# A's masked products in one piece with B's and the state part, keys and slots an iteration sooner in seven steps, values and gates an iteration later

## The chip, the core and the metric

The kernel runs on one core of a Trainium2 chip. The metric is the device time of one execution in microseconds (us); lower is better. The core has five engines with queues of their own: TensorE (PE, with its weight loads shown apart as PEld), VectorE (DVE), ScalarE (ACT), GpSimd (POOL) and SyncE (SP, which issues DMAs here). Each engine takes its instructions in a fixed order; semaphores make one wait for another.

## What is computed

All data are float32. The program is a feed-forward layer with two experts, an attention with a slot memory (16 heads, key width 64, value width 128, 64 slots), and the same feed-forward layer again. The attention of one head, cut to what matters:

```python
z = cumlogsumexp(s, axis=time)            # s: clipped slot scores
p, g = exp(s - z), exp(z[t-1] - z[t])
hk = hk * g[None, :] + k[:, None] * p[None, :]   # key state, step by step
ok = q @ hk;  pv = softmax(ok)                   # over the 64 slots
hv = hv * g[:, None] + p[:, None] * v[None, :]   # value state
o = pv @ hv                                       # then normalised, gated, projected by Wo
```

Two sequences of 1024 tokens with 512 features come in; q, k, s, v and the gate are products of the normalised tokens with five weight matrices.

## The kernel before

The attention works in units: one batch, one group of 4 heads, one chunk of 128 tokens. There are 2 x 4 x 8 = 64 units, taken by a loop over `i` (line 1315 on). In iteration `i` three units are at work: `cur` (unit i) has its keys, slots and queries made, `mid` (unit i-1) has its attention worked out, and `old` (unit i-2) is projected. Before and after the loop stand the two feed-forward layers; the second one starts inside the last iterations.

For one unit the chunk form needs two masked 128 x 128 products for each head. A (line 1117, `scores`) is keys times queries, made at the end of the iteration in which the unit is `cur`, and used by `slot_scores` in the next iteration (PE tile `ok<-A,E`). B (line 1199, `slot_weights`) is slots times softmax weights, made while the unit is `mid`, and used by `outputs` (PE tiles `ov<-v,B` and `svp<-v,B`). Both contract over 64 rows only, so each matmul fills half of the array's rows (form `64*128`), and the two halves run side by side. Their results lie in PSUM tiles of the tag `at` (2 buffers), and DVE multiplies each by the causal mask (line 1114), which also moves it to SBUF. `state_outputs` (`ov<-sv,uT`, `svp<-sv,uT`) has the same half-height form. `value_state_products` (`svp<-v,E`) and the second part of `slot_scores` (`ok<-A,E`) write 64 of 128 columns (form `128*64`). All the rest is `128*128`.

Values with gates and keys with slots are products of 256 tokens (a pair of units) with a 512-row weight, each done as seven block products instead of eight, by sums of blocks made beforehand (a Winograd form). The sums of the tokens (`token_sums`, PE input X) are four DVE additions. Both are generators that are advanced a step at a time between the other work, by the letters handed to `project(even, odd)`: `values_gates` has six steps, `keys_slots` five. Keys of a pair are made in the even iteration of its first unit. The first four steps of values are made in the odd iteration before, the other two in the even iteration:

```python
            project("k", "v")      # then slot_scores(mid)
            project("k", "v")      # then transpose_out(old), slot_softmax(mid)
            project("kvk", "v")    # then transpose_u(mid), update_key_state(mid)
            project("vk", "v")     # then slot_weights(mid), state_outputs, value_state_products
```

After these come `transpose_keys_slots(cur)` (PE tile tk, copied to kET by ACT), `running_sum(cur)` (DVE scans CT and the reciprocal rC), `queries(cur)` every fourth unit (PE tile pq), `outputs(mid)`, `scores(cur)` and `project_out(old)` (PE tile po, added to x by DVE, line 1282).

The order of PE's instructions in the attention is written out by hand: `on_pe` (line 952) chains each matmul behind the one before. The other engines' orders and the choice of a buffer are made by a scheduler that goes by priorities; it makes an instruction wait for what its operands and its buffers need, and PSUM is guarded by whole banks of 2 KB per partition. Slots E have three buffers of one tag (line 1046), keys k two, the token sums X share six buffers with other sums. PSUM tiles of the tag `pj` have two: the projections kU, kV, C, V, pq and po take them in turn.

In `keys_slots` before, C (for the first key) and V share a bank (line 1054); V's first product follows U's second. The weights of a group are loaded by SP in iterations c=4 to 7 of the group before it (queries, values and gates, keys and slots, outputs), and the sums of the weights' blocks for the groups 1 to 3 are made by POOL during b=0 (`weight_sums`, twelve items, two steps an iteration).

Of the kernel before, what the change touches and what calls it, by code (L numbers as in the profile page):

```python
# [15 lines left out]
P = 128  # L16
# [33 lines left out]
def tile_macaron(  # L50
# [406 lines left out]
    def ffn(m, views):  # L457
# [140 lines left out]
        def hidden_fast(ps, ck, xT, T, wfc, S, a, sums):  # L598
            w = wfc.rearrange("p (k d h) -> p k d h", k=2, d=2)
            lo, hi = slice(0, 256), slice(256, 512)  # L600
            a += [None] * 4
            for q in range(2):
                nm = f"{ph}_{ps}_{ck}_{q}"
                first, second = ts(q, P), slice(256 + q * P, 256 + (q + 1) * P)
                U = ps2.tile([P, 256], F32, tag="pj", name=f"hU{nm}")
                V = ps2.tile([P, 256], F32, tag="pj", name=f"hV{nm}")
                C = ps1.tile([P, 256], F32, tag="st", name=f"hC{nm}")

                def product(bank, left, right, start):
# [6 lines left out]
                def keep(name):  # L616
                    t = work.tile([P, 256], F32, tag=name, name=f"{name}{nm}")
# [6 lines left out]
                p1 = keep("rC")  # L624
# [214 lines left out]
    class Attention:  # L839
# [19 lines left out]
        def weight_sums(self):  # L859
# [17 lines left out]

            def load(j):
                g, d = j // 3, j % 3
                if d == 2:  # L880
                    return load_w(w_ks[g], f"kw{g}")
                w = large_tile([P, 4, 512], f"gw{g}_{d}")
                for i, src in enumerate((w_v, w_g)):
                    nc.sync.dma_start(
                        out=w[:, 2 * i : 2 * i + 2, :],
                        in_=src[g].rearrange("p (k d n) -> p k d n", k=2, d=2)[:, :, d, :],
                    )
                return w

            w = None  # L890
            for j in range(3 * NG):
                g, d = j // 3, j % 3
                if w is None:
                    w = load(j)
                if d < 2:
                    parts = w[:, 0], w[:, 2], w[:, 1], w[:, 3]
                    to = vg_sums[g].rearrange("p (t d n) -> p t d n", t=4, d=2)[:, :, d, :]
# [47 lines left out]
    def attention(att, then, then_steps, weight_steps):  # L945
# [36 lines left out]
        def values_gates(u):  # L982
# [19 lines left out]

            product(U, a11, B11, True)
            p1 = keep(U, "th", "p1")
            token_sums(u)
# [24 lines left out]
        def keys_slots(u):  # L1030
            pair = u, units[u.n + 1]
            B11, B21, B22, T1, T2, T3, T4 = att.ks[u.b, u.g]
            a11, a12, a21, a22 = halves(u)
            U = ps2.tile([P, 256], F32, tag="pj", name=f"kU{u.nm}")

            def keep(bank, tag):
                t = work.tile([P, 256], F32, tag=tag, name=f"{tag}{u.nm}", bufs=1)
# [1 line left out]
                return t  # L1039

            def key(v):
                v.k = work.tile([P, HG * DK], F32, tag="k", name=f"k{v.nm}")
                return v.k

            def slot(v, bank, other):
# [2 lines left out]
                nc.vector.tensor_scalar(v.E, v.E, -32.0, 32.0, ALU.max, ALU.min)  # L1048
                nc.scalar.activation(v.E, v.E, AF.Exp)

            product(U, a11, B11, True)
            p1 = keep(U, "kp")

            bank = ps2.tile([P, 2, 256], F32, tag="pj", name=f"kV{u.nm}")
            C, V = bank[:, 0], bank[:, 1]
            product(C, a12, B21, True)
            nc.vector.tensor_tensor(key(u), C, p1, ALU.add)
            yield
            product(U, u.S[:, 1], T2, False)
            u2 = keep(U, "ku")  # L1060
            product(V, u.S[:, 0], T1, False)
            p5 = keep(V, "kv")
            yield
            product(V, u.S[:, 3], B22, False)
            slot(u, V, u2)
# [32 lines left out]
        def masked_products(u, name, lT, rT):  # L1098


            m = work.tile([P, HG, P], F32, tag="msk", name=f"{name}{u.nm}", bufs=3)
            pp = [
                ps2.tile([P, NPR, P], F32, tag="at", name=f"{name}p{u.nm}_{j}") for j in range(2)
            ]
            for pr in range(NPR):
                for j in range(2):
                    r = slice(j * 64, (j + 1) * 64)
                    on_pe(
                        nc.tensor.matmul,
                        pp[j][:, pr, :], lhsT=lT[r, pr, :], rhs=rT[r, pr, :],  # L1110
                        start=True, stop=True,
                    )
            for j in range(2):
                nc.vector.tensor_tensor(m[:, ts(j, NPR), :], pp[j], causal[:, 0:NPR, :], ALU.mult)  # L1114
            return m

        def scores(u):

            u.A = masked_products(
                u, "A", u.kET[:, 0:NPR, :], u.qT[:, :, ts(u.c % 4, P)]  # L1120
            )

        def running_sum(u, prev):

# [63 lines left out]
        def transpose_u(u):  # L1188
# [10 lines left out]
        def slot_weights(u):  # L1199

            u.Bm = masked_products(u, "B", u.kET[:, NPR:, :], u.uT)

# [94 lines left out]

        n = len(units)  # L1300
        norm = att.norm(1)
        ahead = keys = None

        def project_ahead(i):
            nonlocal ahead
            if ahead is None and i % 2 and i + 1 < n:
                ahead = values_gates(units[i + 1])
            if ahead is not None:  # L1310
                next(ahead)

        for _ in range(4):
            project_ahead(-1)
        for i in range(n + 2):
            cur = units[i] if i < n else None
            mid = units[i - 1] if 1 <= i <= n else None
            old = units[i - 2] if i >= 2 else None


            def project(even, odd):
                if i >= n - 1:
                    next(then_steps)
                for step in (odd if i % 2 else even) if cur else "":
                    if step == "v":
                        project_ahead(i)
                    else:
                        next(keys)

            if cur and i % 2 == 0:  # L1330
                keys = keys_slots(cur)
            project("k", "v")
            if mid:
                slot_scores(mid)
            project("k", "v")
            if old:
                transpose_out(old)
            if mid:
                slot_softmax(mid)
            project("kvk", "v")  # L1340
            if mid:
                transpose_u(mid)
                update_key_state(mid)
            project("vk", "v")
            with tc.issue_after(att.pe.ins):
                then.settle()
            if mid:
                slot_weights(mid)
                state_outputs(mid)
                value_state_products(mid)  # L1350
            if cur:
                transpose_keys_slots(cur)
                running_sum(cur, mid)
                queries(cur, mid)
            project("", "")
            if cur and i % 2 == 0:
                ahead = None
            if mid:
                outputs(mid)
                update_value_state(mid)  # L1360
# [1 line left out]
                if mid.b == 0 and mid.c < 6 and mid.g < NG - 1:  # L1362
                    with tc.issue_after(mid.gated.ins):
                        next(weight_steps)
                        next(weight_steps)
            if cur:
                scores(cur)
            if old:
                project_out(old)
            if cur:  # L1370
# [8 lines left out]
                if cur.c >= 4 and cur.n + NC < n:  # L1379
                    v = units[cur.n + NC]  # L1380
                    if cur.c == 4:
                        att.load_queries(v.b, v.g)
                    elif cur.c == 5:
                        att.load_values_gates(v.b, v.g)
                    elif cur.c == 6:
                        att.load_keys_slots(v.b, v.g)
                    else:
                        att.load_outputs(v.b, v.g)
                if cur.g == NG - 1 and cur.b == B - 1:
# [83 lines left out]
```

## Time and profile before

| what | value |
|---|---|
| median of 3 runs | 2323.75 us (2321.03 to 2326.47) |
| the profiled execution | 2324.62 us |
| its span (first to last instruction) | 2322.8 us |
| granted TensorE clock | 0.995 |
| 0 to 496 us (first layer) | PE busy 460.36, DVE 277.74 |
| 496 to 1800 us (attention) | PE busy 1287.17 of 1304.00, DVE 802.10, ACT 518.61, POOL 126.67 |
| 1800 to 2322 us (end of attention, second layer) | PE busy 496.69, DVE 275.66 |

The profile's page lists busy time by engine, the waits by who released whom, and the instructions in order of time. A row of the timeline has the start in us, the time from the first start to the last end in us, the engine, the line, the operation, output<-input, the form, and how many records are merged in it. A float32 matmul shows as two records, a transpose as one. The line of PE's attention work is always 954, that of the helper, so one goes by tiles. The end of a matmul is modelled: 128x512 records last 592 ns and follow each other every 429 ns, so the last 163 ns of each run beside the next one.

### The profile page before, as it was taken

How to read it: one execution, taken by the hardware profiler on the slowest of the kernel's cores; microseconds unless marked ns; L12 is line 12 of the kernel's file. 1: busy time of each engine (PE TensorE's matmuls, PEld its weight loads, DVE VectorE, ACT ScalarE, POOL GpSimd, SP SyncE). 2: the span in 40 equal slices, each digit the busy share in tenths (PEclk: the TensorE clock that was granted, in tenths of full speed). 3: DMA queues.
4: the chain of work that ended last, by engine and by line, in shares of the span. 5: the costliest groups of instructions: out<-in, count | busy, mean ns of one | idle time of the engine just before them, and what ended most of it. 6: DMA issues, size and time to landing. Idle time of an engine off the chain costs nothing.

```text
span 2322.8 us, 28879 instructions
## 1 busy us (share of the span) xinstructions
PE 2244.2 (97%) x10776; PEld 1542.2 (66%) x10776; DVE 1355.5 (58%) x3124; ACT 783.6 (34%) x1526; POOL 470.5 (20%) x400
## 2 busy tenths in 40 slices
PE   6999999999999999999999999999999999999998
PEld 5687787875656656556666655665655667888765
DVE  6544556656656656657765655655656666665411
ACT  2222222323344334334434443343433332222222
POOL 3523615301101101100101000000001245434000
PEclk9999999999999999999999999999999999999999
DMA  7516425231311311310411200210010203323442
GB/s 290 223 55 213 181 88 223 105 116 37 125 53 64 123 46 64 116 56 25 164 33 56 76 32 20 73 42 29 36 37 20 90 33 145 113 96 100 168 172 100
DMA packets 56940, 222.74 MB, mean 96 GB/s; under 512 B 5983, under 2 KB 13151, under 8 KB 38880
## 3 DMA queue, kind: packets, MB, share of 16 engines
q1 hardware_dynamic: 51232, 203.52, 24.7%
q0 software_dynamic: 5280, 16.85, 1.8%
q8 instruction: 85, 1.39, 0.2%
q10 hardware_dynamic: 288, 0.52, 0.1%
q14 instruction: 55, 0.45, 0.1%
HBM read 189.86 MB, written 31.54 MB: 95 GB/s over the span
## 4 chain that ended last, share of the span: by engine, by line
PE 67%; issue 12%; DVE 12%; POOL 3%; ACT 2%; DMA 2%; SPq 0%; POOLq 0%; DVEq 0%; ACTq 0%
PE U L954 8%; PE oa L678 6%; PE hU L611 6%; PE po L954 5%; PE o L678 4%; PE pq L954 4%; PE V L954 4%; PE hp L514 3%; PE op L733 3%; PE hV L611 3%; PE kV L954 3%; PE kU L954 2%; PE C L954 2%; DVE rC L1132 2%; PE svp L954 2%
## 5 line engine op out<-in xcount | busy, mean ns | idle before, releaser
L1240 POOL TENSOR_TENSOR sg<-sg,ms 128x512 f32<-128x512 f32 x64 | 69.0, 1077 | 1178.2 <-DVE ms L1238 1080.1
L954 PE MATMUL po<-wo,oT 128*128 128x512 f32 x512 | 236.7, 605 | 1.7 <-DVE A L1114 1.7
L954 PEld LDWEIGHTS po<-wo,oT 128*128 128x128 f32 x512 | 92.0, 189 | 101.3 <-issue 91.8
L514 PE MATMUL hp<-xsT,wfc 128*128 128x256 f32 (+1 forms) x768 | 148.9, 349 | 10.3 <-DMA wfc<-in_w_fc_dram 5.7
L514 PEld LDWEIGHTS hp<-xsT,wfc 128*128 128x128 f32 x768 | 127.5, 192 | 33.3 <-issue 13.7
L733 PE MATMUL op<-wp,a 128*128 128x512 f32 x320 | 143.2, 593 | 0.0
L1236 ACT ACT_TABLE_LOAD x63 | 80.8, 1283 | 176.7 <-DVE ms L1235 176.6
L501 DVE SCALAR_TENSOR_TENSOR t<-hp,r 128x256 f32<-128x256 f32 (+1 forms) x96 | 36.4, 379 | 154.6 <-ACT r L500 151.0
L954 PE MATMUL U<-vgT,X 128*128 128x512 f32 x256 | 120.7, 594 | 0.0
L1132 DVE RECIPROCAL rC<-CT 128x256 f32<-128x256 f32 x64 | 112.2, 1753 | 2.2
L954 PE MATMUL pq<-xnT,wq 128*128 128x512 f32 x256 | 112.5, 592 | 0.0
L611 PE MATMUL hU<-xsT,wfc 128*128 128x256 f32 x384 | 100.3, 383 | 0.4 <-ACT e L618 0.3
L733 PEld LDWEIGHTS op<-wp,a 128*128 128x128 f32 x320 | 59.7, 190 | 60.9 <-issue 57.9
L1233 DVE TENSOR_REDUCE ms<-sq 128x4 f32<-128x512 f32 x64 | 41.2, 644 | 78.2 <-ACT sq L1231 78.2
L500 ACT ACTIVATE r<-hp 128x256 f32<-128x256 f32 (+1 forms) x96 | 33.2, 347 | 155.4 <-PE hp L514 151.8
L954 PEld LDWEIGHTS pq<-xnT,wq 128*128 128x128 f32 x256 | 47.4, 190 | 53.6 <-issue 53.6
L611 PEld LDWEIGHTS hU<-xsT,wfc 128*128 128x128 f32 x384 | 72.4, 191 | 13.9 <-issue 3.0
L1165 ACT ACT_TABLE_LOAD x63 | 80.8, 1283 | 1.1
L954 PEld LDWEIGHTS U<-vgT,X 128*128 128x128 f32 x256 | 48.9, 191 | 47.9 <-issue 46.2
L1000 ACT ACTIVATE th<-sg 128x512 f32<-128x512 f32 x64 | 40.4, 631 | 112.8 <-DVE sg L998 108.3
L1127 DVE TENSOR_TENSOR_SCAN CT<-ones,CT,kET 128x128 f32<-128x128 f32 x112 | 48.1, 471 | 51.5 <-ACT kET L1096 51.5
L1269 ACT ACTIVATE oT<-to,gnh 128x512 f32<-128x512 f32 x64 | 44.0, 687 | 94.4 <-PE to L954 85.4
(302 smaller groups left out, 5146.9 us busy)
## 6 DMA issues: line engine op xcount, KB each, us to landing
wfc<-in_w_fc_dram SPq DMA_DIRECT2D x48, 1024.0 KB, 5.7
wp<-in_w_proj_dram SPq DMA_DIRECT2D x48, 1024.0 KB, 6.6
vgT<-vgs SPq DMA_DIRECT2D x16, 1024.0 KB, 5.9
wv<-in_w_v_dram SPq DMA_DIRECT2D x8, 1024.0 KB, 7.3
ksT<-kss SPq DMA_DIRECT2D x8, 1024.0 KB, 5.3
wo<-in_w_o_dram SPq DMA_DIRECT2D x8, 1024.0 KB, 4.8
xs<-xs SPq DMA_DIRECT2D x6, 1032.0 KB
wks<-in_w_ks_dram SPq DMA_DIRECT2D x24, 256.0 KB, 3.9
```

Source lines behind the costliest of these rows:

```text
L514: m.mark = nc.tensor.matmul(hp, lhsT=wfc[:, dc * HQ + hc * P : dc * HQ + (hc + 1) * P], rhs=xT[:, dc, :], start=(dc == 0), stop=(dc == DC ...
L611: m.mark = nc.tensor.matmul(bank, lhsT=left[:, d, :], rhs=right[:, d, :], start=start and d == 0, stop=d == 1, skip_group_check=True,)
L678: nc.tensor.matmul(bank[:, t, :], lhsT=left(q)[:, ts(t, P)], rhs=right(q), start=first and q == 0 and (t == 0 or last), stop=last and q == ...
L733: nc.tensor.matmul(ops[j], lhsT=a[hc][:, ts(j, P)], rhs=wp[:, ts(hc, D)], start=(ck == 0 and hc == 0), stop=(ck == NHQ - 1 and hc == HQ // ...
L954: att.pe = op(*args, **kw)
L1127: nc.vector.tensor_tensor_scan(u.CT[:, pr, :], ones, u.kET[:, NPR + pr, :], prev.CT[:, pr, P - 1 : P] if u.c else 0.0, ALU.mult, ALU.add,)
L1132: nc.vector.reciprocal(u.rC, u.CT)
L1165: nc.scalar.activation(u.u, u.u, AF.Exp)
L1233: nc.vector.tensor_reduce(ms, sq, AX.X, ALU.add)
L1236: nc.scalar.activation(ms, ms, AF.Sqrt, bias=eps, scale=1.0 / DV)
L1240: u.gated = then.gated = nc.gpsimd.tensor_tensor(sg, sg, ms.to_broadcast([P, HG, DV]), ALU.mult)
L1269: nc.scalar.activation(u.oT, tp, AF.Copy, scale=gnh)
```

## The change

- `masked_products` now makes B of `mid` and A of `cur` in one go: B's four products, the four of `state_outputs(mid)`, A's four products, then the four masks. A and B of the same half lie in one PSUM tile of 2 KB, so `at` still has two tiles. This happens once in an iteration, before `value_state_products(mid)`.
- For A to be there so soon, keys and slots of a pair are made in the odd iteration before it (`keys_slots(units[i + 1])`), in seven steps instead of five. Those of the first pair are made ahead of the loop, all seven steps in a row. `transpose_keys_slots` and `running_sum` are of unit i+1 now and stand at the end of the iteration; `queries(cur)` stands after the second `project`.
- Values and gates of a pair start in the even iteration of its first unit (four steps); their last two steps fall into the odd iteration after it.
- In `keys_slots` U and V share a bank, and C has its own. V's first product comes ahead of U's second. `token_sums` moves from the first step of values to the first step of keys. k has three buffers instead of two; E keeps three.
- In iterations c=5 and c=6 of a group the loads change places: keys and slots first. `weight_sums` takes the key-and-slot item of a group first. In the feed-forward layer p1 is kept in the tags `kp` and `kv`, one buffer each, instead of `rC`.

```diff
             product(U, a11, B11, True)
             p1 = keep(U, "kp")
-
-            bank = ps2.tile([P, 2, 256], F32, tag="pj", name=f"kV{u.nm}")
-            C, V = bank[:, 0], bank[:, 1]
+            token_sums(u)
+            yield
+            C = ps2.tile([P, 256], F32, tag="pj", name=f"kC{u.nm}")
             product(C, a12, B21, True)
             nc.vector.tensor_tensor(key(u), C, p1, ALU.add)
             yield
+            product(V, u.S[:, 0], T1, False)
+            p5 = keep(V, "kv")
+            yield
             product(U, u.S[:, 1], T2, False)
             u2 = keep(U, "ku")
-            product(V, u.S[:, 0], T1, False)
-            p5 = keep(V, "kv")
             yield
...
+            if u:
+                products(0, u.kET[:, NPR:, :], u.uT)
+                state_outputs(u)
+            if v:
+                products(1, v.kET[:, 0:NPR, :], v.qT[:, :, ts(v.c % 4, P)])
+            if u:
+                u.Bm = mask(0, "B")
+            if v:
+                v.A = mask(1, "A")
...
-            project("k", "v")
+            project("v", "kk")
             if mid:
                 slot_scores(mid)
-            project("k", "v")
+            project("v", "k")
+            if cur:
+                queries(cur, mid)
...
-            project("kvk", "v")
+            project("v", "kvk")
...
-            project("vk", "v")
+            project("v", "vk")
             with tc.issue_after(att.pe.ins):
                 then.settle()
+            if cur or mid:
+                masked_products(mid, cur)
             if mid:
-                slot_weights(mid)
-                state_outputs(mid)
                 value_state_products(mid)
-            if cur:
-                transpose_keys_slots(cur)
-                running_sum(cur, mid)
-                queries(cur, mid)
-            project("", "")
+            project("", "k")
             if mid:
                 outputs(mid)
                 update_value_state(mid)
...
-            if cur:
-                scores(cur)
+            if i + 1 < n:
+                transpose_keys_slots(units[i + 1])
+                running_sum(units[i + 1], cur)
...
                     elif cur.c == 5:
+                        att.load_keys_slots(v.b, v.g)
+                    elif cur.c == 6:
                         att.load_values_gates(v.b, v.g)
-                    elif cur.c == 6:
-                        att.load_keys_slots(v.b, v.g)
```

The order in which the built kernel's instructions stand from the masked products on, by the tiles' names (kU T3, kU T4 and so on are the step's block product; U, V, C without k are those of values):

```
even i   PE   V wg | B x4, state x4, A x4 | svp<-v,E x4 | ov,svp<-v,B x4 | tk x4 | po x4 | kU, kC
         DVE  uT, sk, sg add (V+u2), sg scale (th), B, B, A, A, ms reduce, CT, ms, CT, ms, rC, ms, ms, x add
odd i    PE   U T4, kU T3 | B x4, state x4, A x4 | svp<-v,E x4 | kU T4 | ov,svp<-v,B x4 | tk x4 | po x4 | U, ok, C
         DVE  uT, sk, B, B, E add (kU+kv), A, E clip, A, ms reduce, CT, ms, CT, ms, rC, ms, ms, x add
```

In even iterations with `mid.c` = 5 one token sum stands between the gate's scaling and B as well; with `mid.c` = 7 there is no `svp<-v,E`. The first mask waits for A's product in the same bank; the masks of A have no wait of their own. The second slot addition of a pair (`E add`, odd i) writes the buffer of the slots of unit i-1, and waits for `svp<-v,E` of that unit; kU T4 waits for that addition.

More of the change, by code (lines that the diff above doesn't have):

```diff
@@ L614, in product, with keep @@
                         )
-                def keep(name):
-                    t = work.tile([P, 256], F32, tag=name, name=f"{name}{nm}")
+                def keep(name, bufs=2):
+                    t = work.tile([P, 256], F32, tag=name, name=f"{name}{nm}", bufs=bufs)
                     nc.scalar.copy(t, U)
@@ L623, in hidden_fast @@
                 product(U, w[:, 0, :, first], xT[:, 0:2, lo], True)
-                p1 = keep("rC")
+                p1 = keep(("kp", "kv")[q], 1)
                 product(V, S[0][:, :, first], T[0], True)
@@ L879, in load @@
                 g, d = j // 3, j % 3
-                if d == 2:
+                if d == 0:
                     return load_w(w_ks[g], f"kw{g}")
@@ L885, in load @@
                         out=w[:, 2 * i : 2 * i + 2, :],
-                        in_=src[g].rearrange("p (k d n) -> p k d n", k=2, d=2)[:, :, d, :],
+                        in_=src[g].rearrange("p (k d n) -> p k d n", k=2, d=2)[:, :, d - 1, :],
                     )
@@ L894, in weight_sums @@
                     w = load(j)
-                if d < 2:
+                if d > 0:
                     parts = w[:, 0], w[:, 2], w[:, 1], w[:, 3]
-                    to = vg_sums[g].rearrange("p (t d n) -> p t d n", t=4, d=2)[:, :, d, :]
+                    to = vg_sums[g].rearrange("p (t d n) -> p t d n", t=4, d=2)[:, :, d - 1, :]
                     T = sum_tile([P, 3, 512], f"G{g}_{d}")
@@ L1033, in keys_slots @@
             a11, a12, a21, a22 = halves(u)
-            U = ps2.tile([P, 256], F32, tag="pj", name=f"kU{u.nm}")
+            bank = ps2.tile([P, 2, 256], F32, tag="pj", name=f"kU{u.nm}")
+            U, V = bank[:, 0], bank[:, 1]
             def keep(bank, tag):
@@ L1041, in key @@
             def key(v):
-                v.k = work.tile([P, HG * DK], F32, tag="k", name=f"k{v.nm}")
+                v.k = work.tile([P, HG * DK], F32, tag="k", name=f"k{v.nm}", bufs=3)
                 return v.k
@@ L1096, in transpose_keys_slots, with masked_products, products, mask @@
             nc.scalar.copy(u.kET, tp)
-        def masked_products(u, name, lT, rT):
-            m = work.tile([P, HG, P], F32, tag="msk", name=f"{name}{u.nm}", bufs=3)
+        def masked_products(u, v):
+            nm = (u or v).nm
             pp = [
-                ps2.tile([P, NPR, P], F32, tag="at", name=f"{name}p{u.nm}_{j}") for j in range(2)
+                ps2.tile([P, 2, NPR, P], F32, tag="at", name=f"AB{nm}_{j}") for j in range(2)
             ]
-            for pr in range(NPR):
-                for j in range(2):
[L1107 to L1111, printed above, removed]
-                    )
[L1113 to L1121, printed above, removed]
+            def products(i, lT, rT):
+                for pr in range(NPR):
+                    for j in range(2):
+                        r = slice(j * 64, (j + 1) * 64)
+                        on_pe(
+                            nc.tensor.matmul,
+                            pp[j][:, i, pr, :], lhsT=lT[r, pr, :], rhs=rT[r, pr, :],
+                            start=True, stop=True,
+                        )
+            def mask(i, name):
+                m = work.tile([P, HG, P], F32, tag="msk", name=f"{name}{nm}", bufs=3)
+                for j in range(2):
+                    nc.vector.tensor_tensor(
+                        m[:, ts(j, NPR), :], pp[j][:, i], causal[:, 0:NPR, :], ALU.mult
+                    )
+                return m
+            if u:
[7 more added lines that the diff above has]
+                v.A = mask(1, "A")
         def running_sum(u, prev):
@@ L1197, in transpose_u @@
             nc.vector.tensor_tensor(u.uT, tp, u.rC, ALU.mult)
-        def slot_weights(u):
-            u.Bm = masked_products(u, "B", u.kET[:, NPR:, :], u.uT)
         def state_outputs(u):
@@ L1301, in attention @@
         norm = att.norm(1)
[L1302 to L1314, printed above, removed]
+        values = None
+        for _ in keys_slots(units[0]):
+            pass
+        transpose_keys_slots(units[0])
+        running_sum(units[0], None)
         for i in range(n + 2):
@@ L1324, in project @@
                 for step in (odd if i % 2 else even) if cur else "":
[L1325 to L1328, printed above, removed]
+                    steps = keys if step == "k" else values
+                    if steps:
+                        next(steps)
             if cur and i % 2 == 0:
-                keys = keys_slots(cur)
-            project("k", "v")
+                values = values_gates(cur)
+            elif cur:
+                keys = keys_slots(units[i + 1]) if i + 1 < n else None
+            project("v", "kk")
             if mid:
                 slot_scores(mid)
-            project("k", "v")
+            project("v", "k")
+            if cur:
+                queries(cur, mid)
             if old:
@@ L1343, in attention @@
                 update_key_state(mid)
-            project("vk", "v")
+            project("v", "vk")
             with tc.issue_after(att.pe.ins):
                 then.settle()
+            if cur or mid:
+                masked_products(mid, cur)
             if mid:
-                slot_weights(mid)
-                state_outputs(mid)
                 value_state_products(mid)
-            if cur:
-                transpose_keys_slots(cur)
-                running_sum(cur, mid)
-                queries(cur, mid)
-            project("", "")
-            if cur and i % 2 == 0:
-                ahead = None
+            project("", "k")
             if mid:
```

1 line of the change is left out of this document (removed).

## The prediction

> **What bounds the kernel now.** I read the page's busy times first, then PE's waits, then the timeline of one pair of iterations, engine by engine.
>
> ```profile
> PE 2244.2 (97%) x10776; PEld 1542.2 (66%) x10776; DVE 1355.5 (58%) x3124; ACT 783.6 (34%) x1526; POOL 470.5 (20%) x400
> ```
>
> PE is the bound, so a gain has to come off PE's own row: fewer or quicker matmuls, or fewer waits of PE. Its waits:
>
> ```profile
> PE kV L954 <- DVE k L1057: 8.2, 23, 0.9
> ...
> PE po L954 <- DVE A L1114: 1.7, 1, 1.7
> ```
>
> The columns are total us, times, longest. Only the first recurs. Now PE through one odd iteration:
>
> ```profile
> 1031.69 1.88 PE L954 MATMUL U<-vgT,X 128*128 128x512 f32 x4
> 1033.40 0.38 PE L954 MATMUL tu<-ident,e 128*128 128x128 f32 x2
> ...
> 1034.07 1.88 PE L954 MATMUL V<-wg,X 128*128 128x512 f32 x4
> 1035.88 0.71 PE L954 MATMUL Bp<-uT,kET 64*128 64x128 f32 x8
> 1036.53 0.66 PE L954 MATMUL svp<-v,E 128*64 128x128 f32 x8
> 1037.11 0.33 PE L954 MATMUL tk<-ident,k 128*128 128x128 f32 x1
> ...
> 1038.28 0.39 PE L954 MATMUL svp<-v,B 128*128 128x128 f32 x2
> 1038.59 0.71 PE L954 MATMUL Ap<-qT,kET 64*128 64x128 f32 x8
> 1039.24 3.70 PE L954 MATMUL po<-wo,oT 128*128 128x512 f32 x8
> 1042.78 0.49 PE L206 MATMUL ln<-ident,xr 128*128 128x128 f32 x3
> ```
>
> Read the starts: busy time hides the loss. U's four records take 33.40 - 31.69 = 1.71 us and go from one full-size product to another. V's four, which go to the half-height B, take 1.81. po's eight, which come from the half-height A, take 3.54 where eight at 0.43 make 3.43. So each change of form costs about 0.1 us on either side of it, and no wait is shown for it.
>
> **What the change removes.** (1) A's run of its own. In: svp<-v,B x2 takes 0.31 us, the pairs before it 0.22: 0.09. The run itself: A takes 0.65 to po's start; within one half-height run a pair of records comes every 0.11, so four pairs are 0.45: 0.20. Out: po's 0.11. Together 0.40 us; behind the state part, A costs its 0.45 alone, and the exit that the state part has already moves behind it. 63 of the 65 places have both parts: 63 x 0.40 = 25 us. Bounds: 0.30 and 0.40 each, 19 to 25.
>
> The rule that speaks of this is in the Trainium skill, "TensorEngine Tiling (Array Packing)", Key Properties: a change of the tiling mode drains the array, a change of tile within a mode does not. It gives no time, and the 0.1 us on each side are this trace's.
>
> (2) The wait of V's first key product for k, since C leaves V's bank:
>
> ```profile
> 626.52 1.13 PE L954 MATMUL kU<-ksT,X 128*128 128x256 f32 x4
> ...
> 627.36 0.41 DVE L1057 TENSOR_TENSOR k<-kV,kp 128x256 f32<-128x256 f32 x1
> ...
> 627.83 1.13 PE L954 MATMUL kV<-ksT,X 128*128 128x256 f32 x4 [0.17 <-DVE k L1057]
> ```
>
> k ends at 627.77, and kV starts 0.06 later. The shown idle of 0.17 starts at the modelled end, 0.16 after the place where the next matmul could have gone, and a restarted 256-wide product loses 0.10 more (kV lasts 0.96 to the next start, not 0.86). So 8.2 + 23 x 0.26 = 14 us; bounds 8 (the shown idle alone) and 14. (3) po's single wait for A, 1.7 us, since po no longer follows A. Removed: 25 + 14 + 2 = 41 us.
>
> **What it adds.** Four things, each a wait of PE. Let T be the start of B's first record. From B, PE needs 0.55 for B, 0.45 for the state part, 0.45 for A, 0.10 to leave, and 0.58 for svp<-v,E (1036.53 to 1037.11): it stands at T+2.13.
>
> (a) Even iterations, outputs behind the gate. This is what DVE and ACT do at this place now, with T = 1035.88:
>
> ```profile
> 1036.06 0.69 DVE L998 TENSOR_TENSOR sg<-V,u 128x512 f32<-128x512 f32 x1 [1.20 <-PE V L954]
> 1036.66 0.74 DVE L1114 TENSOR_TENSOR B<-Bp,causal 128x256 f32<-128x256 f32 x2
> 1037.44 0.69 DVE L1001 SCALAR_TENSOR_TENSOR sg<-th,sg 128x512 f32<-128x512 f32 x1
> ```
>
> ```profile
> 1036.78 0.63 ACT L1000 ACTIVATE th<-sg 128x512 f32<-128x512 f32 x1 [2.59 <-DVE sg L998]
> ```
>
> Today the masks of B fill the time in which ACT works out the tanh. In the new order the gate's scaling stands ahead of them: DVE idles until T+1.56, scales, and starts B at T+2.17 (a 0.69 us operation frees DVE after 0.61). B's halves end at T+2.58 and T+2.93. The first output product starts at T+2.63, 0.50 late, and the second half costs 0.07 more: 0.57 for mid.c = 1 and 3. With mid.c = 5 one token sum (0.34) stands in between as well: 0.91. With mid.c = 7 there is no svp<-v,E to cover 0.58: 1.15. Mean 0.80; 31 places give 25 us. If DVE lets the masks through sooner, the least is 0.35; the most is 1.0 where layer norm also stands in the queue: 11 to 31. Behind the late products wait tk, po and the next iteration on PE.
>
> Even without the scaling ahead, the masks come late: the Trainium skill, "PSUM — Partial Sum Buffer", under "PSUM bank collisions raise a hardware error", says to guard PSUM by bank and quadrant, not by address. B's half can therefore not be read while A's is written. By that rule alone B would start at about T+1.65 and only mid.c = 7 would wait, some 0.6 us in 8 places, 5 us instead of 25; the built order has both.
>
> (b) Odd iterations, keys behind slots. Four units' slots now live at once in three buffers, so the last E addition waits for svp<-v,E. DVE does the two B masks first (T+1.63 and T+1.97; the last A product in the bank ends at T+1.60), so the addition starts at T+2.31, lasts 0.41 (the row E<-kU,kv, x32, mean 413 ns), and kU T4 goes at T+2.77, not T+2.13: 0.64, of which nothing is hidden, since the outputs stand behind kU T4. 31 places: 20 us. Without the masks ahead it is 0.58 (18 us); with 0.10 for the restart and a busier DVE 0.80 (25 us). Four E buffers would remove it all.
>
> (c) Odd iterations, kC behind po's addition. kC's bank is po's, as kV's was, and kV pays 0.08 there now (kU's four last 0.94, from 623.49 to 624.43 in the stretch shown above, not 0.86). In the new order scans, reciprocal rC (1.75), the square root on ACT with its table load (1.28 + 0.30) and two small operations stand on DVE ahead of x. From the first output product: squares done 1.53, reduce to 2.13, scans and ms to 3.2, ACT to 4.87, two small ones to 5.22, x to 5.91, kC at 5.96; PE is there after 0.90 + 0.44 + 3.43 + 0.86 = 5.63. That is 0.33 instead of 0.08: 31 x 0.25 = 8 us, between 0 (DVE quicker) and 12.
>
> (d) The seven key steps of the first pair in a row: two copies and an addition each stand between dependent products, about 0.6 us each, and the first softmax has less cover: 3 us, 0 to 6.
>
> The loads that change places: keys and slots (1.75 MB) an iteration sooner, values and gates (3.5 MB) an iteration later, each still one whole iteration (17.7 to 20.4 us) ahead of its use; wv lands 7.3 us after issue, vgT 5.9. SP's queue holds the query load behind them, needed one iteration later. I cost these at nothing; that iteration hides them, and a rival prices the cover's loss. POOL's weight sums are only reordered; POOL is 126.67 us busy of 1304. Moving p1 to kp and kv changes no count. Queries move ahead of the softmax in every fourth unit; their 16 records fill PE as before.
>
> **Sum.** 25 + 20 + 8 + 3 - 41 = +15 us on the span of 2322.8, 2338. The profiled run is 2324.62, 0.9 above the median; on the median, 2323.75 + 15 = 2339 us. The likeliest case's own range takes the ends halfway: 2329 to 2351. A measurement of this kernel can tell about 0.2% (4.6 us) from no change.
>
> **Rivals.** *The gate does not hold the masks* (chance 0.12): DVE's queue gets to B by T+1.7, (a) falls to the 5 us of mid.c = 7. Then 2339 - 20 = 2319. It decides if the mean wait at ov is under 0.15 us ((25 - 20) / 31). Against it: the scaling stands first, and its start at T+1.56 is in the trace.
>
> *It comes out even* (0.09): form changes save 25, V's wait 14, and (b) and (c) stay at 18 and 0 with (a) at 20: 2323.75 + 18 + 20 + 3 - 41 = 2324.
>
> *The late load* (0.05), slower still: at each of 7 group changes values' first product waits for wv and vgT, because the load of c=6 is held until the old group's products are done. Its loads (wv 7.3 us from issue to landing, two of vgT 5.9 each, wg of half vgT's size, about 3 as an estimate) make 22 us one after the other in SP's queue against the 17.7 us of an iteration: some 5 us late, 7 x 5 = 35, so 2374. For it: SP's waits for buffers in the second batch; against: no load shows in PE's waits of the attention now.
>
> *My case* has 0.74. Slower in all: 0.74 + 0.05 = 0.79; same 0.09; faster 0.12. The range 2322 to 2352 leaves out the late load, most of the faster rival and the likeliest case's upper end.
>
> **What would show it.** Right: PE's waits list kU <- DVE E (about 31 times, near 0.5 each as shown), ov <- DVE B (about 31 times), kC <- DVE x; kV <- DVE k is gone; A follows the state part with no gap, and po's eight records after tk take 3.43. Wrong: if A's first record comes 0.2 after the state part, (1) is void; if ov and kU T4 show no wait, time falls to about 2294 (2339 - 25 - 20); if DMA releases appear at U or C, the late load is right.

## The result and the profile after

| kernel | median us | runs | ratio to before, 95% interval |
|---|---|---|---|
| before | 2326.45 (2321.03 to 2328.65) | 13 | |
| after | 2332.11 (2329.91 to 2339.35) | 13 | 1.0032 (1.0022 to 1.0042) |

The changed kernel is slower: by 5.7 us by the medians, by 5 to 10 us by the interval of the ratio. Its profiled run has a span of 2330.4 us against 2322.8, that is 7.6 us more, at the same granted clock (0.996 against 0.995). PE's busy time on the page of the changed kernel:

```profile
PE 2223.0 (95%) x10776; PEld 1538.4 (66%) x10776; DVE 1344.2 (58%) x3124; ACT 788.5 (34%) x1526; POOL 469.0 (20%) x400
```

PE is busy for 21.2 us less with the same 10776 records, and yet the span grows: more than the gain comes back as idle time of PE. Its waits (total us, times, longest) name the places:

```profile
PE kU L954 <- DVE E L1047: 20.7, 33, 1.0
PE ov L954 <- DVE B L1122: 20.1, 28, 1.0
...
PE ts L954 <- DVE sT L1166: 3.1, 5, 0.8
...
PE kC L954 <- DVE x L1292: 1.0, 4, 0.4
```

The wait of kV for k is gone. Two new ones stand at the top, each in about 30 places, which is once in a pair of iterations. The first, in an odd iteration, on PE and then on DVE:

```profile
1080.85 0.71 PE L954 MATMUL AB<-uT,kET 64*128 64x128 f32 x8
...
1081.74 0.27 PE L954 MATMUL svp<-sv,uT 64*128 64x128 f32 x1
1081.85 0.61 PE L954 MATMUL AB<-qT,kET 64*128 64x128 f32 x8
1082.39 0.66 PE L954 MATMUL svp<-v,E 128*64 128x128 f32 x8
1083.63 1.13 PE L954 MATMUL kU<-ksT,xnT 128*128 128x256 f32 x4 [0.58 <-DVE E L1047]
```

```profile
1082.49 0.76 DVE L1122 TENSOR_TENSOR B<-AB,causal 128x256 f32<-128x256 f32 x2 [2.47 <-PE AB L954]
1083.16 0.41 DVE L1047 TENSOR_TENSOR E<-kU,kv 128x256 f32<-128x256 f32 x1
```

A's products (AB<-qT,kET) follow the state part with no gap. The last record of svp<-v,E starts at 1082.77, and where nothing is late the next product starts 0.20 us behind it (e1_four_slots below), so kU T4 could go at 1082.98. It goes at 1083.63, 0.06 us after the slot addition has ended at 1083.57. The addition itself has stood behind both masks of B on DVE, which had been idle for 2.47 us before them. The second wait, in an even iteration, DVE first and then PE:

```profile
1062.26 0.69 DVE L1001 SCALAR_TENSOR_TENSOR sg<-th,sg 128x512 f32<-128x512 f32 x1 [0.69 <-ACT th L1000]
1062.87 0.75 DVE L1122 TENSOR_TENSOR B<-AB,causal 128x256 f32<-128x256 f32 x2
```

```profile
1062.24 0.66 PE L954 MATMUL svp<-v,E 128*64 128x128 f32 x8
1063.35 0.49 PE L954 MATMUL ov<-v,B 128*128 128x128 f32 x2 [0.45 <-DVE B L1122]
```

The gate's scaling waits for ACT's tanh, B's masks wait behind the scaling, and the output product starts 0.07 us after B's first half.

### The profile page after: what moved, and what is told of

It is laid out like the page before. It is cut to its first block, busy times and chain, and to the rows that moved or that the text cites. A ratio compares the mean times of both kernels' runs of the same rounds, so it can differ in the third digit from the quotient of the medians.

```text
span 2330.4 us, 28928 instructions
## 1 busy us (share of the span) xinstructions
PE 2223.0 (95%) x10776; PEld 1538.4 (66%) x10776; DVE 1344.2 (58%) x3124; ACT 788.5 (34%) x1526; POOL 469.0 (20%) x400
## 4 chain that ended last, share of the span: by engine, by line
PE 72%; DVE 18%; issue 5%; ACT 2%; DMA 1%; POOL 1%; SPq 0%; another core or an unknown queue 0%; POOLq 0%; DVEq 0%; ACTq 0%
PE U L954 9%; PE kU L954 6%; PE oa L678 6%; PE hU L611 6%; PE V L954 5%; PE pq L954 5%; PE po L954 5%; PE o L678 4%; PE hp L514 4%; PE hV L611 3%; PE op L733 3%; PE C L954 2%; PE ok L954 2%; DVE rC L1146 2%; PE ov L954 2%
## 5 line engine op out<-in xcount | busy, mean ns | idle before, releaser
L954 PE MATMUL po<-wo,oT 128*128 128x512 f32 x512 | 230.4, 593 | 0.0
L954 PE MATMUL kU<-ksT,X 128*128 128x256 f32 x384 | 103.9, 393 | 1.1 <-DVE E L1047 0.6
L1176 DVE TENSOR_REDUCE mx<-ts 128x4 f32<-128x256 f32 x64 | 27.0, 421 | 124.6 <-PE ts L954 124.6
L954 PEld LDWEIGHTS kU<-ksT,X 128*128 128x128 f32 x384 | 67.7, 189 | 28.2 <-issue 12.7
L1122 DVE TENSOR_TENSOR B<-AB,causal 128x256 f32<-128x256 f32 x128 | 48.2, 418 | 60.2 <-PE AB L954 60.0
```

Of the source, the lines that this page charges most:

```text
L954: att.pe = op(*args, **kw)
L1122: nc.vector.tensor_tensor(m[:, ts(j, NPR), :], pp[j][:, i], causal[:, 0:NPR, :], ALU.mult)
```

## The experiments

Where a time is taken from "the starts of PE's records", it is the sum of the distances from each record to the next of the kind named, in one profiled run against another. Where an edit leaves a kind of the attention alone, most of these sums agree within some 0.1 us between two traces, and a few differ by up to 1 us. One stretch has to be kept apart: from 496 to 536 us the profile shows a granted clock of 0.91 in e3_both, e6_a_before_state and e8_c_late, and of 1.00 in all the other kernels. From the first product of the attention to the first tu it takes these three 38.0 to 38.4 us, and the other kernels with the changed order 34.4 to 36.8.

**Four slot buffers (e1_four_slots).** The changed kernel with

```diff
-                v.E = work.tile([P, HG * M], F32, tag="E", name=f"E{v.nm}", bufs=3)
+                v.E = work.tile([P, HG * M], F32, tag="E", name=f"E{v.nm}", bufs=4)
...
-            u2 = keep(U, "ku")
+            u2 = keep(U, "kp")
```

> The changed kernel with four slot buffers instead of three (the copy u2 shares p1's buffer to make room). Theory: the second slot addition no longer waits for svp<-v,E, so it runs ahead of B's masks, and kU T4 goes at once. 31 places x 0.65 us = 20 us: about 2312 against the changed kernel's 2332, and the wait of kU for E is gone. Rival (the wait only covers another one, so that B's masks or the products behind kU T4 are late next): at most half of it, 2322 or more, with a new wait at ov in the odd iterations.

2311.16 us, ratio 0.9947 (0.9932 to 0.9962): 21 us under the changed kernel, as the theory had it. The step from svp<-v,E to kU T4 falls from 28.1 to 6.3 us over its 31 places, and no other kind of the attention moves by more than 0.4 but for one single step of the first pair (1.0). PE and then DVE at the same place of this kernel:

```profile
1072.39 0.71 PE L954 MATMUL AB<-uT,kET 64*128 64x128 f32 x8
...
1073.93 0.66 PE L954 MATMUL svp<-v,E 128*64 128x128 f32 x8
1074.52 1.13 PE L954 MATMUL kU<-ksT,xnT 128*128 128x256 f32 x4
```

```profile
1072.50 0.42 DVE L1047 TENSOR_TENSOR E<-kU,kv 128x256 f32<-128x256 f32 x1 [1.00 <-PE kU L954]
...
1074.03 0.75 DVE L1122 TENSOR_TENSOR B<-AB,causal 128x256 f32<-128x256 f32 x2 [0.78 <-PE AB L954]
```

The addition now runs in time that was idle, and B's masks are no later than they were: they start 1.64 us after B's first product in both kernels (1074.03 - 1072.39, 1082.49 - 1080.85).

**The buffer or the queue (e5_queue).** One buffer more did two things: it took away a wait and it changed DVE's order. So the order is put back by hand, with four buffers kept:

```diff
                 u.Bm = mask(0, "B")
+                if late:
+                    with tc.issue_after(u.mask_ins):
+                        late()
```

Here `late` holds the second slot addition of the pair with its clip and exponential.

> The kernel of e1_four_slots (four slot buffers) with the second slot addition put behind B's masks on DVE by hand. It tells the buffer from the queue. Theory (the buffer mattered because it sent the addition behind the masks, which wait for A's products): kU T4 is late again, by the same 0.65 us in 31 places, and the time goes back from 2311 to about 2331. Rival (the wait is for the buffer itself, that is for svp<-v,E): with a buffer free nothing is late, 2311.

2335.52 us, ratio 1.0039 (1.0026 to 1.0052): the whole 20 us are back, and so is the line:

```profile
PE kU L954 <- DVE E L1047: 20.4, 33, 0.9
```

So DVE's order alone makes the whole wait, and a free buffer with that order gains nothing. The reverse, three buffers with the addition put ahead of the masks, was not run. There the addition would still have to follow svp<-v,E of the unit whose buffer it takes, and in the changed kernel it starts only 0.12 us after the modelled end of the last such record in 27 places and 0.48 after it in four. By these figures the better order alone would gain about 5 us of the 22 at most (an estimate). The fourth buffer is what makes the better order possible.

**The gate's scaling behind the masks (e2_gate_late).** The changed kernel with

```diff
+                def scale():
-                nc.vector.scalar_tensor_tensor(v.sg, th, 1.0, v.sg, ALU.add, ALU.mult)
+                    nc.vector.scalar_tensor_tensor(v.sg, th, 1.0, v.sg, ALU.add, ALU.mult)
+                v.scale = scale
...
                 masked_products(mid, cur)
+            if cur and i % 2 == 0:
+                with tc.issue_after(cur.mask_ins):
+                    cur.scale()
```

> The changed kernel with the gate's scaling, and nothing else, put behind the masks on DVE. Theory: ov waits because the scaling stands ahead of B. In the changed kernel's trace this costs 28 us. B's masks then wait for A's products in their bank alone: the second half is still some 0.2 us late in 24 places (5 us) and the places without svp<-v,E keep some 0.6 us each (7 x 0.6 = 4 us). So 28 - 9 = 19 us less: about 2313. Rival (B is late for the bank alone, whatever stands ahead of it): 0 to 5 us less, 2327 to 2332, and ov's wait stays.

2319.33 us, ratio 0.9976 (0.9968 to 0.9985): 13 us less, two thirds of what was expected. The wait of ov on the list falls from 20.1 us in 28 places to 6.7 in 13:

```profile
PE ov L954 <- DVE B L1125: 6.7, 13, 0.5
```

By the starts of PE's records the outputs behind svp<-v,E lose 10.7 us (19.1 to 8.4 in 24 places) and those with mid.c = 7 lose 3.7 (9.2 to 5.5 in 7). Left are 3.6 and 4.0 us of wait. The 28 us of the expectation had also counted the slower start of the first output product (about 0.1 us in 31 places), which is no wait: it is the price of leaving the half-height form, and it stays wherever the exit stands.

**Both (e3_both).** The two edits together.

> The changed kernel with four slot buffers and the gate's scaling behind the masks. Theory: the two waits lie in different iterations (odd and even) and add up: 20 + 19 = 39 us less, about 2293, some 33 us under the kernel before (2326). Rival (a third wait comes to light, such as kC behind po's addition or the softmax's chain): 2303 or more.

2302.81 us, ratio 0.9899 (0.9884 to 0.9915). The two come close to adding up (21 + 13 = 34 us; measured 29 by the medians, 31 by the ratios), and the result is 1% faster than the kernel before. In the profiled run both steps fall by the same amounts as alone (28.1 to 6.3, 19.1 to 8.4 and 9.2 to 5.5 us), and the stretch at the granted clock of 0.91 takes 4.0 us more than in the changed kernel. The result lies on the rival's bound of 2303. The gate's smaller part accounts for 6 of the 10 us that are missing against 2293; the wait for x stood in the changed kernel already and does not grow by more than 0.7 us.

**A's products apart again (e4_split).** From e3_both, so that the two waits are out of the way; the gate's scaling then stands behind B's masks of itself, ahead of A's products:

```diff
-            if cur or mid:
-                masked_products(mid, cur)
+            if mid:
+                masked_products(mid, None)
...
                 running_sum(units[i + 1], cur)
+            if cur:
+                masked_products(None, cur)
             if old:
```

> The kernel of e3_both with A's four products apart again, in a run of their own ahead of po, and all else the same. Theory: a run of its own costs 0.40 us in 63 places: 25 us more than e3_both, about 2318. Rival (the changes of form are hidden, and the gain of the change comes from V's bank alone): within 5 us of e3_both.

2308.83 us, ratio 0.9938 (0.9922 to 0.9954): slower than e3_both, but by 6 us and not by 25. Neither was right. An odd iteration of each shows the price of the run by itself, first e3_both and then e4_split:

```profile
1069.35 0.71 PE L954 MATMUL AB<-uT,kET 64*128 64x128 f32 x8
...
1073.77 3.60 PE L954 MATMUL po<-wo,oT 128*128 128x512 f32 x8
```

```profile
1070.87 0.71 PE L954 MATMUL AB<-uT,kET 64*128 64x128 f32 x8
...
1075.58 3.70 PE L954 MATMUL po<-wo,oT 128*128 128x512 f32 x8
```

From B to po it is 4.42 against 4.71 us, and po lasts 3.60 against 3.70: 0.39 us, the 0.40 of the prediction. Over all places the starts of PE's records give 25 us for the separate run. But the separate run gives something back elsewhere: the products of keys (6.3 us), the outputs after svp<-v,E (3.6), those with mid.c = 7 (2.3) and the distances among outputs (3.0), and the scores' transposes (2.6). The slot scores, in turn, lose 3.0 us, which fits A's coming later there. So A in one piece with B has two prices. It holds B's masks, which the prediction had put mostly under the gate's scaling: the 8.9 us at the outputs. And PE comes sooner to kC: this product starts 0.25 us late in 22 of the 26 places where po comes right before the keys, and 0.08 us late in 25 of them with A apart, as in the kernel before.

**A ahead of the state part (e6_a_before_state).** That price, tested from e3_both by one line moved:

```diff
             if u:
                 products(0, u.kET[:, NPR:, :], u.uT)
-                state_outputs(u)
             if v:
                 products(1, v.kET[:, 0:NPR, :], v.qT[:, :, ts(v.c % 4, P)])
             if u:
+                state_outputs(u)
                 u.Bm = mask(0, "B")
```

> The kernel of e3_both with A's products ahead of the state part (B, A, state in place of B, state, A), so that the last write to the banks that the masks read comes 0.45 us sooner. Theory (B's masks wait for A in the same bank): ov's wait in six places of mid.c=5 (3.6 us) and most of the wait in the seven places of mid.c=7 (0.58 us each, 4.0 us) go, and part of the second half's (up to 2.8 us): 7 to 10 us less than e3_both's 2303, about 2294. Rival (the masks are late because DVE is busy): no change, 2303.

2291.51 us, ratio 0.9853 (0.9839 to 0.9867): 11 us less, just above what was expected. By the starts of PE's records the outputs lose 7.5 us of lateness (2.8 after svp<-v,E, 2.7 with mid.c = 7, 2.0 at the second half). In e2_gate_late, where the state part comes first, PE and DVE stand so:

```profile
1053.47 0.61 PE L954 MATMUL AB<-qT,kET 64*128 64x128 f32 x8
```

```profile
1054.12 0.76 DVE L1125 TENSOR_TENSOR B<-AB,causal 128x256 f32<-128x256 f32 x2 [0.77 <-PE AB L954]
```

and in this kernel:

```profile
1046.32 0.61 PE L954 MATMUL AB<-qT,kET 64*128 64x128 f32 x8
```

```profile
1046.96 0.75 DVE L1125 TENSOR_TENSOR B<-AB,causal 128x256 f32<-128x256 f32 x2 [0.32 <-PE AB L954]
```

In both, the masks of B start 0.64 to 0.65 us after A's first product, although B's own products were done 0.45 us sooner in the first. DVE was idle before both (0.77 and 0.32 us), so the rival is out. The masks follow the last write into the bank, not the last write into B, as the kernel's waits make them.

**C behind the slot scores (e8_c_late).** From e6, one step of keys later:

```diff
-            project("v", "kk")
+            project("v", "k")
             if mid:
                 slot_scores(mid)
-            project("v", "k")
+            project("v", "kk")
```

> The kernel of e6_a_before_state with C's key product moved behind the slot scores, so that po's addition has some 1.4 us more to free its bank. Theory: kC's wait for x and its restart go, 7.8 + 2.8 us in the trace of e3_both, and ok follows kU with no wait: 8 to 10 us under e6, about 2285, the fastest of all. Rival (the bank's wait moves on to the next user of the two, or the slot scores' chain is late for k): within 3 us of e6.

2280.73 us, ratio 0.9802 (0.979 to 0.9815), the fastest of all and 2% under the kernel before. The distances between products of keys fall by 10.1 us, as the theory had it, and the scores' transposes come 2.9 us sooner, which was not foreseen. C's product now stands between the slot scores and these transposes, which would cover part of the scores' way through DVE; that was not tested apart. PE's share on its page:

```profile
PE 2212.8 (97%) x10776; PEld 1540.1 (68%) x10776; DVE 1344.0 (59%) x3124; ACT 789.1 (35%) x1526; POOL 468.2 (21%) x400
```

PE is busy 97% of the time, as in the kernel before, with 31 us less to do.

**V's bank alone (e7_v_late, e9_v_after_to).** Term (2) by itself, in the kernel before, by one more `yield` between U's second and V's first product. First with the last key step put behind the queries (`project("k", "")` in place of `project("", "")`):

> The kernel before, with V's first key product one step later (six steps instead of five, and the last key step behind the transposes of keys), so that it comes long after the key addition in its bank. Nothing else of the change. Theory: the wait of V for k and its restart, 0.58 us on the mean in 24 places, goes: 14 us under before, about 2311. Rival (only the idle time that the profile shows is worth anything): 8 us, 2318. If the later last step makes E or the transposes late, it is less.

2346.39 us, ratio 1.0075 (1.0062 to 1.0088): 20 us slower by the medians and 17 by the ratio, with a wide spread (2338.70 at a granted clock of 0.995, 2348.58 at 0.991). V's wait is gone, but the list of waits has two others:

```profile
PE pq L954 <- ACT qT L1089: 11.0, 16, 0.7
...
PE ts L954 <- DVE sT L1153: 5.6, 14, 1.5
```

The first was not foreseen. kU keeps one of the two buffers of `pj` until its last step; with that step behind the queries, both halves of the queries share the other buffer, and the second half waits for the copy of the first. The second fits the cover that V's product had given to the scores' transposes: their step behind the outputs' transposes grows by 11.1 us. So V was moved again, with the last step left where it was:

```diff
             u2 = keep(U, "ku")
+            yield
             product(V, u.S[:, 0], T1, False)
...
                 transpose_out(old)
+            if i < n - 1:
+                project("k", "")
...
-            project("kvk", "v")
+            project("vkk", "v")
```

> The kernel before with V's first key product moved behind the transposes of old's outputs, half a microsecond later, and the step after it behind values' fifth; the last key step stays where it was, ahead of the queries, unlike e7_v_late. Theory: the wait of V for k (12.3 us by the starts of PE's records) and the restart of its 256-wide product (2.5 us) go, the queries wait for no bank: 14 us under before, about 2311. Rival 1 (only the shown idle of 8 us counts): 2318. Rival 2 (the transposes of scores, which V's product covered in part, wait for sT as in e7_v_late): 3 to 11 us come back, 2314 to 2323.

2317.81 us, ratio 0.9970 (0.9959 to 0.9981): 7 us faster. By the starts of PE's records the 12.3 us ahead of V are gone, as expected, and the wait of kV for k with them. But the slower start of V's first product stays (2.2 of 2.5 us, now behind the transposes), and the transposes of outputs, which V had covered, are late by about 4 us in all. V's second product, which had stood behind the scores' transposes and now follows a product of 512 columns, loses a slow start of 2.8 us that the theory had not counted. Over all products of the attention the trace has 10.5 us less, and 3.4 us more in the two layers, which the edit does not touch. The theory had the wait right and the restart wrong; the rival of 2318 has the right time for another reason, since the whole wait did go.

## Why the prediction was right

The prediction had the sign, both new waits with their places and sizes, and the two gains, and the time came out 7 us lower than 2339, inside its range. The step itself came out at less than half: +5.7 us by the medians and +7.6 by the spans of the profiled runs, where +15 was worked out. That 2332 lies as near to 2339 as it does is in part luck: the sum had been set on 2323.75, the median of three runs, and the kernel before came to 2326.45 over thirteen, from which the same sum gives 2341. The terms come off better than their sum. All products of the attention together take 12.1 us more in the profiled run, and the products of the two layers 4.7 us less, for which the sum had no term. Step by step, with what the records of the changed kernel give against those of the kernel before:

| step | predicted us | measured us |
|---|---|---|
| (1) A's run of its own | -25 | -25 (e4_split); -22 with the exits |
| (2) V's wait for k | -14 | -14.8 |
| (3) single waits | -2 | -1.7 for A, -2.8 for x |
| (a) outputs behind the gate | +25 | +25 |
| (b) keys behind slots | +20 | +22 |
| (c) kC behind po's addition | +8 | +5 |
| (d) the first pair | +3 | -1, within the spread |
| ts behind sT, not foreseen | 0 | +3 |

(1) Each separate run costs 0.39 us, as worked out. That a change of mode drains the array, the rule taken from the Trainium skill, "TensorEngine Tiling (Array Packing)", Key Properties, agrees with this; the price is the runs', and that a drain is what costs it no run shows. The 3 us that are missing in the changed kernel are the exits: leaving a half form costs the next product about 0.10 us where that is ov or kU, and only 0.055 where it is the short transpose tk, as before. This was not priced.

(2) Ahead of V's first key product the records lose 12.3 us and its slower first product 2.5. Alone, in e9_v_after_to, it was worth 7 us (10.5 in the attention's products of the trace); there V had to be moved into a place where it covered other waits, so the numbers are not of the same edit.

(a) The size is right: 14.3 us ahead of ov behind svp<-v,E, 7.7 in the seven places with mid.c = 7, 2.8 at the second half. The single places agree as well: ov behind svp<-v,E is late by 0.52 us in 14 places and by 1.07 in 7, and by 1.11 where mid.c = 7, against 0.50, 0.84 and 1.08 worked out. The working, however, gave nearly all of it to the scaling. e2_gate_late and e6_a_before_state split it: with the scaling out of the way, 10 us of it stay, some 8 of them because the masks wait for A's products in the same bank (8.9 us go in e4_split, 7.5 in e6_a_before_state). The prediction had 5 us for that, at mid.c = 7 alone. The kernel's waits keep to the rule cited from the Trainium skill, "PSUM — Partial Sum Buffer", under "PSUM bank collisions raise a hardware error": in both stretches shown the masks start behind A's products. Whether the chip could read B's half sooner was not tried.

(b) 0.66 us in 27 places and 1.02 in four, 21.8 in all, against 0.64 predicted in 31. The prediction put 0.58 on the wait for svp<-v,E alone and 0.64 on the masks ahead. e5_queue shows that the masks ahead make the whole wait by themselves, and that a free buffer behind them is worth nothing.

(c) was too dear. Ahead of kC 7.1 us are lost where 2.2 were lost at the same place before. In 26 places po comes right before the keys, and there kC is late by 0.25 us in 22 and by 0.34 to 0.53 in four, against 0.08 before: near the 0.33 and 0.08 worked out. But there are 26 such places and not 31. In four more, layer norm's transposes stand between po and kU, and kC does not wait at all.

(d) The first transposes of u come at 531.2 us against 532.3, but this says little: from the first product of the attention to there it takes 34.4 us in the changed kernel and 34.4 to 36.8 in the other runs of its order at the same granted clock. A cost of 3 us is neither shown nor ruled out.

The range does not follow from the prediction's own bounds: with every term halfway to its end they give 2325 to 2354 and not 2329 to 2351. The measured time lies in both.

The table's last column adds up to +13 us (with -22 for the first row), the attention's products to +12.1, the layers' to -4.7, and the ends of the records differ by 7.7 (2313.8 and 2321.5 us). Of the layers' part 2.6 us stand at the second layer's transposes `lt` among the attention's products: 4.5 to 6.5 us in the three traces of the old order, 1.9 in all eight of the new one. The rest is of the size by which untouched stretches of the layers vary from trace to trace (the end of the second one takes 415.4 to 417.4 us), and stays unassigned.

Of the rivals, "the gate does not hold the masks" is out: its scaling stands ahead of them in the trace, and moving it gained 13 us. "It comes out even" is out by the interval, though the +5.7 us lie nearer to its 0 than to the +15; its terms are out too, since (a), (b) and (c) came to 25, 22 and 5 us where it had 20, 18 and 0. "The late load" is out: no DMA is among the releasers of the attention's products in the changed kernel.

## What to carry to other kernels

When work is joined into one run on the engine that bounds, ask what reads the results and where that reader stands in its own queue: here 25 us of form changes were won and some 45 lost at two places where PE waits for DVE, and four small edits of order and buffers turned a loss of 0.3% into a gain of 2%. Results that share a bank are ready for their reader when the last of them is written, so write what is read later elsewhere or sooner. A buffer count can decide an order: when a tile waits for its buffer, look at what the scheduler lets pass ahead of it. A gain and a loss of 40 us each leave a small difference, so its sign hangs on every term.

## What the runs showed that was not expected

A product of 256 columns can start slowly without a wait. In the kernel before, V's first product takes 0.32 us from its first record to its second, and not 0.22, in the 24 places where it waited, and 0.22 in the seven where it followed kU without a wait. But kU takes 0.32 in all 31 places behind `ok<-A,E`, and V's second product 0.29 on the mean behind the scores' transposes, and neither waited. In e9_v_after_to V's first product, now behind the outputs' transposes, takes 0.32 in 10 places, eight of them behind a wait, about 0.28 in 7 without a wait, and 0.22 in 12. What tells these apart was not tested. So a slow start seen behind a wait need not go when the wait goes.

And one `pj` buffer held for one step longer cost 15 us at the 16 pairs of query products (e7_v_late), more than the wait that the edit removed.
